# A four-layer graph network on one core: where layer 2's load buffers lie, and when the last row groups of layer 1 are updated

## The chip, the core and the metric

The kernel runs on one core of a Trainium2 chip. The core has five engines, each with a stream of instructions of its own: TensorE (PE) multiplies, VectorE (DVE), ScalarE (ACT) and GpSimd (POOL) work elementwise, SyncE (SP) issues most transfers. [...] The metric is the device time of one execution in microseconds (us), as a median of several runs.

## The reference

A graph of N = 2708 nodes has 128 features each (`x`) and a sparse weighted adjacency matrix (`adj`, about 16 neighbours a row). Four layers follow each other, each as `x = x + layer(relu(layernorm(x)), adj)`:

```python
h = jnp.maximum(_layernorm(x, axis=-1), 0.0)
x = x + _L0_gnn_ref(h, adj)          # H.T @ X, scaled by 1 / column sums
h = jnp.maximum(_layernorm(x, axis=-1), 0.0)
x = x + _L1_gnn_ref(h, adj, ...)     # sum over j of gelu(s_i + d_j + b) * adj[i, j], then an update
h = jnp.maximum(_layernorm(x, axis=-1), 0.0)
x = x + _L2_gnn_ref(h, adj, ...)     # adj @ states, a dense layer, a GRU cell
h = jnp.maximum(_layernorm(x, axis=-1), 0.0)
x = x + _L3_gnn_ref(h, adj, ...)     # masked attention with two heads
```

The end of layer 1, which matters here, is for every row

```python
combined = jnp.concatenate([node_feats, aggregated], axis=-1)
new_feats = combined @ upd_w.T + upd_b
h = jax.nn.gelu(new_feats, approximate=False) + node_feats
return (h - mu) / jnp.sqrt(var + LN_EPS) * ln_w + ln_b
```

and then the residual and the layer norm with relu that open layer 2.

## The kernel before

Rows lie in 22 tiles of 128 (the last has 20 rows), and the tiles in six groups: groups 0 to 4 have four tiles, group 5 (`LAST`) has tiles 20 and 21.

Layer 1 uses lists instead of the dense matrix. For every row and each of 22 column blocks the up to eight largest entries are kept: values in `val`, places in `col`. Each row tile then passes through a pipeline of *periods*, one period a tile, written out by hand: the order of instructions on each engine is the order of the calls. `period(t)` has six sub-steps `k` (`GB` = 6). In it PE multiplies for tile t (`combine`, `gather`), while DVE, POOL, ACT and SP prepare tiles t+1 to t+3. The steps named below:

- `pass_on` (line 826): PE transposes `where` (`p_w`), ACT copies it, SP writes it to memory and reads it back to every partition as `spread`.
- `columns` (836): DVE turns `spread` into `cols`, an operand of `combine`.
- `place` (line 773 to 679): DVE makes `where`, `value` and `mine` for the tile two ahead.
- `put_values` (805): POOL makes eight 128x128 blocks of `put`, an operand of `gather`; `put_more` (814): ACT makes the other fourteen.
- `activate` (899): ACT applies gelu to `combine`'s result and so frees its bank.
- `close_tile` (920 to 929): PE ends the tile's sum; after a group's last tile ACT copies it to `aggT`.

When a group's tiles are closed, `mix` (942, 943) multiplies the group's features and `aggT` by the update's weights into `p_u`, and `update` brings the group to the input of layer 2 in eight steps on alternating engines: 0 DVE adds the bias; 1 ACT gelu; 2 DVE adds the features and takes moments, POOL takes a power for the root (line 120); 3 DVE makes factors (126 to 130); 4 ACT scales (136), POOL multiplies and adds `ln_w`, `ln_b` (972); 5 DVE adds to `xs` and takes moments, POOL the power; 6 DVE makes factors; 7 ACT writes the rows of `h` (named `hs` in the profile) that layer 2 multiplies. Every group does one step a period, at sub-step 2, starting the period after its `mix`. So groups 3, 4 and 5 end after the last period: eight more rounds of `updates` follow period 22. Then come a check of the lists' lengths (`over`, `many`, lines 1092 to 1097) and the end of the hand-written order; the pools of layer 1 close, those of layers 2 and 3 open over the freed memory.

In layer 2, for each of six column chunks (512 columns wide, the last 148), SP loads the transposed adjacency (`adjT`) in five pieces of up to five row tiles into three rotating buffers `a` of pool `l2a` (lines 1334, 1336). DVE and POOL write from each piece the byte mask that layer 3 uses (1338, 1341), and PE adds the product with the rows of `h` (1346): 22 row tiles, two recorded products each, 44 a chunk. `finish_chunk` follows, interleaved with the next chunk by a small planner that counts units of PE time. A buffer is loaded again when its mask operations and products are done. Layer 3 runs its attention products on PE.

Memory: a pool gets its place when it opens, and what lies there was used by something else. The first load into a buffer waits for all earlier readers and writers of these bytes. In before, the three `a` buffers lie at bytes 167904 to 198624 of each partition, over the end of layer 1's working tiles: `aggT`, of which the last `mix` reads, lies from 166848 to 168896.

Of the kernel before, what the change touches and what calls it, by code (L numbers as in the profile page):

```python
# [20 lines left out]
F32 = mybir.dt.float32  # L21
# [9 lines left out]
P = 128  # L31
# [29 lines left out]
def listed_layers(ctx: ExitStack, tc: tile.TileContext, x, adj, w, out, flag):  # L61
# [76 lines left out]
    def tiles_of(v, t, k):  # L138
        return [v[:, t + q, :] for q in range(k)]
# [66 lines left out]
    lim = fix.tile([P, 4], F32, name="lim")  # L206
    wheres = [fix.tile([P, P], BF16, name=f"where{q}") for q in range(2)]
    msg_wT, upd_wT = (fix.tile(list(w[v].shape), F32, name=v) for v in ("msg_wT", "upd_wT"))
    upd_b, ln_w, ln_b, msg_b = (fix.tile([P, D], F32, name=v) for v in ("upd_b", "ln_w", "ln_b", "msg_b"))
    src_self = fix.tile([P, 2, D], F32, name="src_self")  # L210
    state = {}

# [259 lines left out]
            )  # L472

    def measure(g):
        state["m", g] = moments(tiles_of(xs, *GROUPS[g]), "n1")

    def rows(g):
        t, k = GROUPS[g]
# [5 lines left out]
    for s in range(1, RING):  # L484
        load_cut(0, s)
    nc.vector.tensor_scalar(offdiag, ident, -1.0, 1.0, ALU.mult, ALU.add)
    state["m", -1] = moments(tiles_of(xs, 0, 4), "n0")
    for q in range(2):
        nc.gpsimd.memset(wheres[q], 0.0)

# [49 lines left out]
    for i, (c, s) in enumerate(order):  # L540
        g0, gk = GROUPS[s]
        if i == len(order) - 1:
            for n in range(4):
                list_last(n)
            count_some(0, FIRST)
            count_some(FIRST, 1)
        list_cut(c, s, g0)
        if i == 0:
            state["f", 0] = factors(*state.pop(("m", -1)))
            list_cut(c, s, g0 + 1)  # L550
            state["m", 1] = moments(tiles_of(xs, *GROUPS[1]), "n0")
            list_cut(c, s, g0 + 2)
            state["f", 1] = factors(*state.pop(("m", 1)))
            list_cut(c, s, g0 + 3)
        else:
            for n in range(g0 + 1, g0 + gk):
                if c > 0 and s == (1 if c < LAST - 1 else 0) and n == g0 + 2:
                    invert(c - 1)
                list_cut(c, s, n)
        if i + 1 < len(order):  # L560
            mask_near(*order[i + 1])
        if i > 0 and i - 1 + RING < len(order):
            load_cut(*order[i - 1 + RING])
        if c == LAST - 2:
            load_cut(LAST, s)
        if c > 0 and s == (2 if c < LAST - 1 else 1):
            turn_sums(c - 1)
        if (c, s) == (LAST - 1, LAST):
            turn_rows(LAST - 2)
            ranked = rank(0, FIRST, bank("p_r"))  # L570
            turn_sums(LAST)
        work_cut(c, s, first_steps(s) if c == 0 else next_steps(c, s))
        if c > 1 and s == 0:
            turn_rows(c - 2)
        if c > 1 and s == 1:
            destinations(c - 2)
        if c > 1 and s == 3:
            split_destinations(c - 2)
        if c == LAST - 1:
            for z in PARTS.get(s, ()):  # L580
                mask_near(LAST, z)
                work_cut(LAST, z)
            if s == LAST - 1:
                for _ in lift(LAST):
                    pass

        if (c, s) == (0, 3):
            nc.sync.dma_start(msg_wT, w["msg_wT"])
            nc.sync.dma_start(upd_wT, w["upd_wT"])
            for v, name in ((upd_b, "upd_b"), (ln_w, "ln_w"), (ln_b, "ln_b"), (msg_b, "msg_b")):  # L590
                nc.sync.dma_start(v, w[name].partition_broadcast(P))
        if (c, s) == (2, 3):
            W_msgT, W_ihT, W_hhT = load(late, "W_msgT"), load(late, "W_ihT"), load(late, "W_hhT")
            b_msg, b_ih, b_hh = load_columns(late, "b_msg"), load_columns(late, "b_ih"), load_columns(late, "b_hh")
            ff0T, ff0, ff1T = load(late, "ff0T"), load(late, "ff0"), load(late, "ff1T")
            attn = load_columns(late, "attn")
            gain1, shift1, gain2, shift2 = (load_columns(late, v) for v in ("g1", "b1", "g2", "b2"))
            nc.gpsimd.tensor_copy(src_self[:, 0, :], msg_wT[:, 0, :])
            nc.gpsimd.tensor_tensor(src_self[:, 1, :], msg_wT[:, 0, :], msg_wT[:, 1, :], ALU.add)
# [60 lines left out]
    with (  # L660
# [284 lines left out]
        def update(g, step):  # L945
            t, k = GROUPS[g]
            if step == 0:
                u = work.tile([P, 4, D], F32, name="u1")
                if g not in mixed:
                    mix(g)  # L950
                if size(t + k - 1) < P:
                    nc.vector.memset(u[:, k - 1, :], 0.0)
                pv = mixed.pop(g).rearrange("p (t d) -> p t d", t=4)
                bv = upd_b.unsqueeze(1).to_broadcast([P, 4, D])
                whole = k if size(t + k - 1) == P else k - 1
                nc.vector.tensor_tensor(u[:, 0:whole, :], pv[:, 0:whole, :], bv[:, 0:whole, :], ALU.add)
                if whole < k:
                    nc.vector.tensor_tensor(u[0:TAIL, whole, :], pv[0:TAIL, whole, :], upd_b[0:TAIL, :], ALU.add)
                ups[g] = [u]
# [17 lines left out]
                scale_rows(tiles_of(h, t, k), tiles_of(xs, t, k), *ups[g].pop(), AF.Relu)  # L977
                ups.pop(g)

        def updates(t):  # L980

            for g, (first, k) in enumerate(GROUPS):
                step = t - (first + k + 1)
                if 0 <= step < STEPS:
                    update(g, step)

        GB = (NB + 3) // 4

        def period(t, between=()):

# [4 lines left out]
            for k in range(GB):  # L995
# [20 lines left out]
                if k == 1:  # L1016
                    if now and t % 2 == 0 and t + 2 < NT:
                        project(t // 2 + 1)
                    for g, (first, n) in enumerate(GROUPS):
                        if t == first + n + 1:  # L1020
                            mix(g)
                if k in (1, 2) and b:
                    fetch(t + 2, k - 1)
                if k == 1 and a:
# [1 line left out]
                if k == 2:  # L1026
                    if now and t % 2 == 0 and t + 2 < NT:
                        sources(t // 2 + 1)
                    if a:
                        select_rows(t + 3)  # L1030
                    if now and t + 4 < NT:
                        count_rows(t + 4)
                    updates(t)
                if k > 0 and c:
                    put_more(t + 1, k)
                if k == 3 and c:
# [43 lines left out]
        if True:  # L1080
            period(0)
            for t in range(1, NT + 1):
                period(t)
            for t in range(NT + 1, NT + 1 + STEPS):
                updates(t)
        ordered.close()
        puts.close()


        over = fix.tile([P, 2], F32, name="over1")  # L1090
        many = once.tile([P, NT, NB], BF16, tag="picked", name="many")
        nc.vector.tensor_tensor(many, ends, rows_n, ALU.add)
        nc.vector.tensor_scalar(many, many, float(E), None, ALU.is_gt)
        nc.vector.reduce_sum(over[:, 0:1], many, AX.XY)
        nc.vector.tensor_scalar(many, val[:, :, :, S - 1], 0.0, None, ALU.is_gt)
        nc.vector.reduce_sum(over[:, 1:2], many, AX.XY)
        nc.vector.tensor_tensor(flag, over[:, 0:1], over[:, 1:2], ALU.add)
    lists.close()


# [1 line left out]

    l3 = ctx.enter_context(tc.tile_pool(name="l3", bufs=1))
    h3 = l3.tile([P, NT, D], F32, name="h3")
    mask = l3.tile([P, NT, N], U8, name="mask")
    below = l3.tile([P, 2 * NT + 1], F32, name="below")
    nc.gpsimd.memset(below, 0.0)
    hv = l3.tile([P, NT, 2, D + 1], F32, name="hv")  # L1110
    lift = l3.tile([P, NT, 2], F32, name="lift")
    row = l3.tile([P, 2, N], F32, name="row")
    score = l3.tile([P, NT, 4], F32, name="score")
    nc.gpsimd.memset(score[:, NT - 1, :], 0.0)
    nc.gpsimd.memset(hv[:, NT - 1, :, :], 0.0)
    nc.gpsimd.memset(lift[:, NT - 1, :], 0.0)
    nc.gpsimd.memset(mask[:, NT - 1, :], 0)
    ident_8 = l3.tile([P, P], U8, name="ident_8")
    nc.vector.tensor_copy(ident_8, ident)
    PIECE = 5  # L1120
    RUNS = ((0, 3), (3, 8), (11, 8), (19, 3))
    MOST = 8
    accs = ctx.enter_context(tc.tile_pool(name="l23p", bufs=1, space=PSUM))


    clock = [0.0]
# [192 lines left out]
            yield apart  # L1319

    with (
        tc.tile_pool(name="l2a", bufs=3) as apool,
        tc.tile_pool(name="l2g", bufs=1) as pool,
        tc.tile_pool(name="l2z", bufs=2) as zpool,
        tc.tile_pool(name="l3v", bufs=4) as vpool,
        tc.manual_schedule(),
    ):
        def aggregate(t0, k0, pa, j0):

# [131 lines left out]

        for g, (t0, k0) in enumerate(GROUPS):
            pa = accs.tile([P, CH], F32, tag=f"acc{g % 2}", name="p_agg")
            for j0 in range(0, NT, PIECE):
                aggregate(t0, k0, pa, j0)
            if t0 == 0:
                late_weights()
            follow(finish_chunk(t0, k0, pa))
            advance()
        last = RUNS[0]  # L1470
        banks = products(last, (0, 1), vpool, 2)

    out_pool = ctx.enter_context(tc.tile_pool(name="l3o", bufs=2))

# [487 lines left out]
```

## Time and profile before

| what | us |
|---|---|
| median of three runs (1040.25 to 1042.27) | 1040.8 |
| the profiled execution | 1038.74 |
| its span, first to last instruction | 1036.9 |
| PE busy in the span | 925.8 |
| DVE busy | 798.5 |
| ACT busy | 533.0 |
| POOL busy | 470.7 |
| mean granted PE clock, as a share of full speed | 0.94 |

The profile's first lines give the busy share of each engine in 40 slices of about 26 us, in tenths (9 stands for 90% or more), then the granted clock of PE:

```profile
PE   5799898945999999999999779999978999999983
DVE  7999798977677888987774456666588977997793
ACT  5755656824666676676666312333322434654342
POOL 6322221422977789897875373344311300340042
PEclk9899899965899999999999789999989999999996
```

Layer 0 fills slices 1 to 9, layer 1 goes on to slice 22, layer 2 from there to slice 29, layer 3 takes the rest. Lines of a timeline give start, length, engine, source line, operation, output<-input, shapes and count of merged instructions; in brackets the engine's idle time before it and what ended it.

### The profile page before, as it was taken

How to read it: one execution, taken by the hardware profiler on the slowest of the kernel's cores; microseconds unless marked ns; L12 is line 12 of the kernel's file. 1: busy time of each engine (PE TensorE's matmuls, PEld its weight loads, DVE VectorE, ACT ScalarE, POOL GpSimd, SP SyncE). 2: the span in 40 equal slices, each digit the busy share in tenths (PEclk: the TensorE clock that was granted, in tenths of full speed). 3: DMA queues.
4: the chain of work that ended last, by engine and by line, in shares of the span. 5: the costliest groups of instructions: out<-in, count | busy, mean ns of one | idle time of the engine just before them, and what ended most of it. 6: DMA issues, size and time to landing. Idle time of an engine off the chain costs nothing. (4 is left out here: it accounts for less than half of the span.)

```text
span 1036.9 us, 22170 instructions
## 1 busy us (share of the span) xinstructions
PE 925.8 (89%) x7948; PEld 748.7 (72%) x7948; DVE 798.5 (77%) x2753; ACT 533.0 (51%) x1561; POOL 470.7 (45%) x588
## 2 busy tenths in 40 slices
PE   5799898945999999999999779999978999999983
PEld 3455455624999999999999634444578999989972
DVE  7999798977677888987774456666588977997793
ACT  5755656824666676676666312333322434654342
POOL 6322221422977789897875373344311300340042
PEclk9899899965899999999999789999989999999996
DMA  9799899512333342433221345566411467456100
GB/s 301 254 307 372 256 384 376 200 58 84 120 107 122 100 128 93 128 95 122 80 93 56 135 163 189 191 222 208 117 48 31 141 212 218 135 162 208 36 14 17
DMA packets 83194, 162.90 MB, mean 157 GB/s; under 512 B 14672, under 2 KB 30148, under 8 KB 83074
## 3 DMA queue, kind: packets, MB, share of 16 engines
q1 hardware_dynamic: 63094, 129.25, 38.5%
q10 hardware_dynamic: 19980, 32.14, 8.5%
q8 instruction: 64, 1.05, 0.4%
q14 instruction: 56, 0.46, 0.2%
HBM read 114.74 MB, written 30.87 MB: 140 GB/s over the span
## 5 line engine op out<-in xcount | busy, mean ns | idle before, releaser
L805 POOL TENSOR_SCALAR put<-count,line,value 128x128 f32<-128x128 f32 x176 | 200.0, 1149 | 32.8 <-DVE value L794 32.6
L1184 PE MATMUL att<-hv,wt 128*128 128x129 f32 x1672 | 195.9, 278 | 7.8 <-DVE wt L1154 6.3
L1184 PEld LDWEIGHTS att<-hv,wt 128*128 128x128 f32 x1672 | 192.2, 194 | 10.8 <-DVE wt L1154 7.0
L887 PE MATMUL p_m<-s,sel 128*128 128x128 bf16 x1452 | 163.3, 221 | 8.8 <-ACT g L899 6.3
L891 PE MATMUL p_m<-d,cols 124*128 124x128 bf16 (+1 forms) x1452 | 163.3, 221 | 2.9 <-DVE cols L836 2.9
L1154 DVE SCALAR_TENSOR_TENSOR wt<-row,lift,mask 128x1024 f32<-128x1024 f32 (+1 forms) x132 | 138.8, 1082 | 23.3 <-PE att L1184 23.3
L120 POOL TENSOR_TENSOR n_r<-n_r,minus_half 128x4 f32<-128x4 f32 (+1 forms) x28 | 39.9, 1425 | 233.3 <-DVE n_r L119 226.1
L912 PE MATMUL agg<-put,g 128*128 128x128 f32 (+1 forms) x968 | 123.1, 279 | 0.0
L1346 PE MATMUL p_agg<-a,hs 128*128 128x512 f32 (+2 forms) x264 | 110.4, 560 | 13.7 <-DMA a<-adjT 7.6
L380 PE MATMUL sums<-a,h 128*128 128x512 f32 x220 | 120.3, 644 | 1.6 <-ACT h L136 1.6
L394 PEld LDWEIGHTS p_T<-ident,a 128*128 128x128 f32 (+1 forms) x440 | 55.9, 147 | 81.5 <-issue 37.5
L912 PEld LDWEIGHTS agg<-put,g 128*128 128x128 f32 x968 | 113.7, 193 | 0.0
L887 PEld LDWEIGHTS <-sel 128*128 128x128 bf16 x1452 | 104.5, 98 | 10.7 <-issue 10.1
L891 PEld LDWEIGHTS <-cols 124*128 124x128 bf16 (+1 forms) x1452 | 103.7, 98 | 3.8 <-DVE cols L836 3.8
L814 ACT ACTIVATE put<-mine,value 128x128 f32<-128x128 bf16 x308 | 100.6, 392 | 0.0
L899 ACT ACTIVATE g<-p_m 128x512 f32<-128x512 f32 x132 | 72.8, 551 | 53.7 <-PE agg L912 41.2
L394 PE MATMUL p_T<-ident,a 128*128 128x128 f32 (+1 forms) x440 | 74.3, 290 | 26.8 <-ACT aT L399 20.2
L1346 PEld LDWEIGHTS p_agg<-a,hs 128*128 128x128 f32 (+1 forms) x264 | 48.0, 195 | 62.7 <-issue 53.1
L358 DVE FIND_INDEX8 col<-val,a 128x8 uint16<-128x124 f32 x342 | 92.0, 281 | 0.0
L356 DVE MAX8 val<-a 128x8 f32<-128x124 f32 x342 | 79.1, 272 | 8.3 <-DMA a<-in_adj 8.3
L399 ACT ACTIVATE aT<-p_T 128x512 f32<-128x512 f32 (+2 forms) x132 | 71.0, 539 | 26.5 <-PE p_T L394 25.4
L1307 ACT ACTIVATE hs<-hs 128x1354 f32<-128x1354 f32 (+1 forms) x44 | 58.4, 1329 | 48.5 <-DMA hs<-in_adj 48.1
(279 smaller groups left out, 1559.3 us busy)
## 6 DMA issues: line engine op xcount, KB each, us to landing
hs<-in_adj SPq DMA_DIRECT2D x42, 677.0 KB
adjT<-aT ACTq DMA_DIRECT2D x105, 256.0 KB
a<-adjT SPq DMA_DIRECT2D x20, 1280.0 KB
spread<-passed SPq DMA_DIRECT2D x22, 704.0 KB
later<-sel SPq DMA_DIRECT2D x22, 616.0 KB
a<-in_adj SPq DMA_DIRECT2D x5, 1152.0 KB
a<-in_adj SPq DMA_DIRECT2D x5, 1120.0 KB
a<-in_adj SPq DMA_DIRECT2D x5, 1088.0 KB
```

The costliest lines, as they stand in the source:

```text
L356: nc.vector.max(val[0:m, n, b, :], v)
L358: nc.vector.max_index(col[0:m, n, b, :], val[0:m, n, b, :], v)
L380: nc.tensor.matmul(accs[c][:, 0:w], h0[0:m, n, :], a[0:m, n - g0, t0 * P - lo : t0 * P - lo + w], start=(n == 0), stop=(n == NT - 1),)
L394: nc.tensor.transpose(p[0:k, i * iw + q * P : i * iw + q * P + m], a[0:m, q, e : e + k], ident[0:m, 0:m])
L805: nc.gpsimd.tensor_scalar(st["put", 0][:, b, :], count, st["line"][:, b : b + 1], st["value"][:, b : b + 1], ALU.is_equal, ALU.mult,)
L814: nc.scalar.activation(st["put", 1][:, b - HP, :], st["mine"][:, b - HP, :], AF.Identity, scale=st["value"][:, b : b + 1])
L887: nc.tensor.matmul(p[:, b - b0, :], st["sel"][:, b, :], s3[:, q, t % 2, :], start=(q == 0), stop=False)
L891: nc.tensor.matmul(p[:, b - b0, :], st["cols"][0:kb, b, :], d3[0:kb, b, q, :], start=False, stop=(q == 2))
L912: nc.tensor.matmul(agg, g[:, b - 4 * k, :], put, start=(b == 0), stop=False)
L1154: nc.vector.scalar_tensor_tensor(wt[:, 0:n], row[:, k, c : c + n], lift[:, j, k : k + 1], mask[:, j, c : c + n], op0=ALU.max, op1=ALU.mult,)
L1184: nc.tensor.matmul(banks[s // 3][:, s % 3, :], wt[:, q * P : (q + 1) * P], hv[:, j, k, :], start=(v < 2 and s // 3 not in touched), stop=( ...
L1346: nc.tensor.matmul(pa[:, 0:n], h[0:k, j, :], a[0:k, j - j0, 0:n], start=(j == 0), stop=(j == NT - 1))
```

## The change

1. The pools of layers 2 and 3 are placed anew. The tiles of layer 3 open at memory's far end (`side="right"`). The load buffers `a` now lie at bytes 52192 to 82912: the first wholly over `val`, the second over the end of `col` and over `later`, the third over the end of `val` and most of `col`. These pools and the PSUM pool `l23p` take `reuse_waits="tile"`. The biases `upd_b`, `ln_w`, `ln_b` move to a pool that lives on, and two sets of small tiles take the name "n4".
2. The list check moves to period 20, sub-step 1, as `check_lists`.
3. `mixes` and `updates` are tables over (period, sub-step). Groups 0 to 2 keep their places. Group 3 does a step every three sub-steps: period 17, sub-step 2, to period 20, sub-step 5. Group 4 is mixed in period 20 at sub-step 3, and does a step every sub-step from there to the end of period 21.
4. Group 5 has no place in the table. Its `mix` and step 0 stand before the first chunk's products, the rest between its five pieces: steps 1 and 2 after the first, 3 and 4 after the second, 5 after the third, 6 and 7 after the fourth. Its tile comes from layer 2's pool `l2z`.
5. Memsets of layer 3's last rows move into the first chunk (the mask's after the third piece, four small ones after the fifth). The hand-written order runs on to the end of layer 2.

```diff
-    upd_b, ln_w, ln_b, msg_b = (fix.tile([P, D], F32, name=v) for v in ("upd_b", "ln_w", "ln_b", "msg_b"))
+    upd_b, ln_w, ln_b = (late.tile([P, D], F32, name=v) for v in ("upd_b", "ln_w", "ln_b"))
+    msg_b = fix.tile([P, D], F32, name="msg_b")
...
-                u = work.tile([P, 4, D], F32, name="u1")
+                u = work.tile([P, 4, D], F32, name="u1") if g < LAST else zpool.tile([P, 4, D], F32, name="z3")
...
-        def updates(t):
-
-            for g, (first, k) in enumerate(GROUPS):
-                step = t - (first + k + 1)
-                if 0 <= step < STEPS:
-                    update(g, step)
-
         GB = (NB + 3) // 4
+        mixes, updates = {}, {}
+        for g, (first, n) in enumerate(GROUPS[:-1]):
+            at, apart = (first + n + 1) * GB + 1, GB
+            if g == LAST - 2:
+                apart = GB // 2
+            elif g == LAST - 1:
+                at, apart = at - GB + 2, 1
+            mixes[divmod(at, GB)] = g
+            for step in range(STEPS):
+                updates.setdefault(divmod(at + 1 + step * apart, GB), []).append((g, step))
+
+        def check_lists():
+            over = fix.tile([P, 2], F32, name="over1")
+            many = once.tile([P, NT, NB], BF16, tag="picked", name="many")
+            nc.vector.tensor_tensor(many, ends, rows_n, ALU.add)
+            nc.vector.tensor_scalar(many, many, float(E), None, ALU.is_gt)
+            nc.vector.reduce_sum(over[:, 0:1], many, AX.XY)
+            nc.vector.tensor_scalar(many, val[:, :, :, S - 1], 0.0, None, ALU.is_gt)
+            nc.vector.reduce_sum(over[:, 1:2], many, AX.XY)
+            nc.vector.tensor_tensor(flag, over[:, 0:1], over[:, 1:2], ALU.add)
...
-                    for g, (first, n) in enumerate(GROUPS):
-                        if t == first + n + 1:
-                            mix(g)
+                if (t, k) in mixes:
+                    mix(mixes[t, k])
...
-                    updates(t)
+                for g, step in updates.pop((t, k), ()):
+                    update(g, step)
+                if k == 1 and t == NT - 2:
+                    check_lists()
...
-            for t in range(NT + 1, NT + 1 + STEPS):
-                updates(t)
-        ordered.close()
+            assert not updates
         puts.close()
...
-    l3 = ctx.enter_context(tc.tile_pool(name="l3", bufs=1))
+    l3 = ctx.enter_context(tc.tile_pool(name="l3", bufs=1, side="right", reuse_waits="tile"))
...
-    accs = ctx.enter_context(tc.tile_pool(name="l23p", bufs=1, space=PSUM))
+    accs = ctx.enter_context(tc.tile_pool(name="l23p", bufs=1, space=PSUM, reuse_waits="tile"))
...
-        tc.tile_pool(name="l2a", bufs=3) as apool,
+        tc.tile_pool(name="l2a", bufs=3, reuse_waits="tile") as apool,
...
         for g, (t0, k0) in enumerate(GROUPS):
             pa = accs.tile([P, CH], F32, tag=f"acc{g % 2}", name="p_agg")
-            for j0 in range(0, NT, PIECE):
+            if g == 0:
+                update(LAST, 0)
+            for i, j0 in enumerate(range(0, NT, PIECE)):
                 aggregate(t0, k0, pa, j0)
-            if t0 == 0:
+                if g > 0:
+                    continue
+                for step in ((1, 2), (3, 4), (5,), (6, 7), ())[i]:
+                    update(LAST, step)
+                if i == 2:
+                    nc.gpsimd.memset(mask[:, NT - 1, :], 0)
+            if g == 0:
+                blank_rows()
+                nc.vector.tensor_copy(ident_8, ident)
                 late_weights()
             follow(finish_chunk(t0, k0, pa))
             advance()
         last = RUNS[0]
         banks = products(last, (0, 1), vpool, 2)
+    ordered.close()
```

More of the change, by code (lines that the diff above doesn't have):

```diff
@@ L474, in measure @@
     def measure(g):
-        state["m", g] = moments(tiles_of(xs, *GROUPS[g]), "n1")
+        state["m", g] = moments(tiles_of(xs, *GROUPS[g]), "n4")
     def rows(g):
@@ L486, in listed_layers @@
     nc.vector.tensor_scalar(offdiag, ident, -1.0, 1.0, ALU.mult, ALU.add)
-    state["m", -1] = moments(tiles_of(xs, 0, 4), "n0")
+    state["m", -1] = moments(tiles_of(xs, 0, 4), "n4")
     for q in range(2):
@@ L550, in listed_layers @@
             list_cut(c, s, g0 + 1)
-            state["m", 1] = moments(tiles_of(xs, *GROUPS[1]), "n0")
+            state["m", 1] = moments(tiles_of(xs, *GROUPS[1]), "n4")
             list_cut(c, s, g0 + 2)
@@ L1083, in listed_layers @@
                 period(t)
-            for t in range(NT + 1, NT + 1 + STEPS):
-                updates(t)
-        ordered.close()
+            assert not updates
         puts.close()
[L1090 to L1097, printed above, removed]
     lists.close()
-    l3 = ctx.enter_context(tc.tile_pool(name="l3", bufs=1))
+    l3 = ctx.enter_context(tc.tile_pool(name="l3", bufs=1, side="right", reuse_waits="tile"))
     h3 = l3.tile([P, NT, D], F32, name="h3")
@@ L1108, in listed_layers @@
     below = l3.tile([P, 2 * NT + 1], F32, name="below")
-    nc.gpsimd.memset(below, 0.0)
     hv = l3.tile([P, NT, 2, D + 1], F32, name="hv")
@@ L1113, in listed_layers, with blank_rows @@
     score = l3.tile([P, NT, 4], F32, name="score")
[L1114 to L1117, printed above, removed]
     ident_8 = l3.tile([P, P], U8, name="ident_8")
-    nc.vector.tensor_copy(ident_8, ident)
+    def blank_rows():
+        for v, to in ((below, 0.0), (score[:, NT - 1, :], 0.0), (hv[:, NT - 1, :, :], 0.0), (lift[:, NT - 1, :], 0.0)):
+            nc.gpsimd.memset(v, to)
     PIECE = 5
@@ L1321, in listed_layers @@
     with (
-        tc.tile_pool(name="l2a", bufs=3) as apool,
[L1323 to L1326, printed above, removed]
+        tc.tile_pool(name="l2a", bufs=3, reuse_waits="tile") as apool,
+        tc.tile_pool(name="l2g", bufs=1, reuse_waits="tile") as pool,
+        tc.tile_pool(name="l2z", bufs=2, reuse_waits="tile") as zpool,
+        tc.tile_pool(name="l3v", bufs=4, reuse_waits="tile") as vpool,
     ):
```

## The prediction

> **What bounds the kernel now.** I read in this order: the 40 slices, then a table of stretches over the seam between layers 1 and 2, then PE, the DMA queue and DVE in order of time. In the slices PE is at 9 tenths or more nearly everywhere and sags to 7 in slices 23 and 24, where the granted clock sags as well. That is the seam.
>
> ```profile
> 583.36:585.60 2.24, 2.13 (x9) 1.32 (x8) 1.52 (x6) 2.20 (x7) 0.00 (x0) 0.50 0.00 0
> 585.60:591.57 5.97, 0.00 (x1) 0.04 (x1) 3.81 (x21) 2.26 (x6) 1.81 (x2) 0.50 0.83 282
> 591.57:606.43 14.86, 14.86 (x30) 6.23 (x30) 11.44 (x30) 2.53 (x6) 11.28 (x13) 0.88 0.41 152
> 606.43:611.89 5.46, 0.00 (x0) 0.03 (x1) 1.88 (x7) 0.88 (x2) 4.12 (x4) 0.71 0.91 301
> 611.89:620.15 8.26, 8.26 (x15) 3.24 (x15) 2.58 (x6) 0.00 (x0) 5.44 (x3) 0.78 0.52 169
> ```
>
> Columns: stretch, its length, busy time of PE, weight load, DVE, ACT, POOL (with counts), granted clock, DMA share, GB/s. From the last product of layer 1 (583.36) to the end of layer 2's first chunk (620.15) pass 36.8 us: the update products `p_u` 2.2, a hole of 6.0, 30 aggregate products in 14.9, a hole of 5.5, the last 14 in 8.3. On both sides of this PE is full (20.00 of 20 us from 540 to 560, 25.82 of 26 from 620 to 646), so what the seam gains or loses moves the end.
>
> ```profile
> 585.56 1.52 SPq L1334 DMA_DIRECT2D a<-adjT  x3
> ...
> 591.57 8.85 PE L1346 MATMUL p_agg<-a,hs 128*128 128x512 f32 x16 [6.08 <-issue]
> ...
> 610.44 0.88 ACT L136 ACTIVATE hs<-xs,n_r 128x128 f32<-128x128 f32 x2 [10.11 <-DVE n_r L130]
> ...
> 611.89 8.26 PE L1346 MATMUL p_agg<-a,hs 128*128 128x512 f32 x14 [5.47 <-DMA a<-adjT]
> ...
> SPq L1334 <- PE p_u L943: 22.2, 1, 22.2
> ```
>
> The first hole: SP held the three load buffers' DMAs for 22.2 us until the last `p_u` product had read its operand, then issued all three; the first landed 6 us later. The second: load 4 was issued only at 605.92 (landed 611.8), and the `h` rows of group 5 were written only at 610.44.
>
> [...] clock 0.50 from 582 to 594, then 1.00; a product takes 0.44 us warm (30 in 13.23 from 633.80), the first 30 take 14.86. [...] Here a DVE mask took 3.35 us beside a POOL memset, 1.22 later; a POOL mask 2.8 beside DVE, 1.49 alone.
>
> **The change part by part.**
>
> *Loads.* In the changed program's order, load 1 waits for DVE's list check, which moves into period 20; loads 2 and 3 wait for the last `cols` on DVE and for POOL's `put` of tile 21. In before these ended by 555.7, 563.3 and 559.3; I reckon 562 and 569 below. A 1.28 MB load took 6 us, so all three land near 578, ahead of the first aggregate, and share no bytes with what PE still reads. The first hole's 6.0 us goes.
>
> *Group 5's update moves between the masks.* PE no longer stands behind the tail of groups 3, 4 and 5. With `p_u` ending at 590.9 (below): row of step 0 ends 591.5, gelu 592.0, mask 1 on DVE 1.6, step 2 1.5, POOL pow 595.3, mask 2, step 3 597.0, ACT 597.9, POOL's two 0.73 after its second mask 599.5, step 5 601.1, POOL mask and pow 603.0, DVE mask 4, step 6 607.0, ACT 607.9. PE wants these rows after 40 products, 590.9+14.9+10x0.44 = 610.2: slack 2.3 us. Load 4 follows PE's tenth product (597) and lands near 603, wanted at 605.8. Both parts of the second hole go, 5.5 us, and the last 14 products run warm: 14x0.44 = 6.2, 2.1 less.
>
> Sum of gains: 6.0+5.5+2.1 = 13.5 us with rounding. The first cold start I leave in (14.86).
>
> *Group 3 now does two steps a period.* Step 2 lands in period 18 ahead of `cols` and `place` on DVE. There DVE has no slack:
>
> ```profile
> 538.49 0.94 DVE L836 TENSOR_SCALAR cols<-spread,part 128x2816 bf16<-128x2816 bf16 x1
> ...
> 541.05 0.34 DVE L793 TENSOR_REDUCE where<-picked 128x22 bf16<-128x176 f32 x1
> ...
> 541.44 0.23 PE L822 MATMUL p_w<-ident_h,where 128*128 128x128 bf16 x1
> ```
>
> PE's `p_w` starts when `where` ends. Step 2 in before ran from 545.33 to 547.97, 2.64 us. PE waits that much: first for `cols`, then for `where`. Bounds: 1.5 (less if DVE drifts ahead) to 3.5 [...]. I take 2.6. Step 3 (0.9) follows `place` and is covered; in period 19 step 2 is gone from DVE, and step 5 comes after `place`. The list check (2.8 us) has DVE's idle 6.65 us before the last `cols` as cover.
>
> *Group 4's steps lie at every sixth of a period.* The mix moves 1.8 us of PE from period 21 to 20: zero. But step 7's four ACT rows now stand in ACT's queue before the two copies of `aggT` that PE's last `p_u` waits for. The chain of group 4 in before, from gelu to the last row, went hand to hand, each wait ended by its own last step:
>
> ```profile
> 583.63 0.64 ACT L963 ACTIVATE u<-u 128x512 f32<-128x512 f32 x1
> ...
> 590.77 1.27 POOL L972 TENSOR_TENSOR u<-u,ln_w 128x512 f32<-128x512 f32 x1 [2.75 <-ACT u L136]
> ...
> 598.68 1.65 ACT L136 ACTIVATE hs<-xs,n_r 128x128 f32<-128x128 f32 x4 [0.85 <-DVE n_r L130]
> ```
>
> 583.63 to 600.33 is 16.7 us. After: the gelu follows period 20's last activate (565.73, plus 2.6 for the stall, plus 1.8 for the mix: 570.1), its own 0.3 and group 3's step 7 (1.65): it starts at 572.1. It ends at 588.8, `aggT` at 589.2. PE wants `aggT` from 583.75+2.6 = 586.4. PE waits 2.7-2.8 us; I take 2.7. Bounds 0 and 5. Queued behind the ACT rows is only this copy; behind it PE's `p_u` and with it all of layer 2.
>
> *POOL.* Ahead of `put` of tile 21 now come group 3's two 128x512 operations (1.3 to 2.0 each) and two pows. `put` of 20 runs 545 to 554, these to 560.4, `put` of 21 to 567.4 or, at its 1.15 us each, 569.6. Its products start near 578: covered. The memsets of layer 3 (0.7 us and the mask's 2.41) move between masks; counted above.
>
> *One answer:* the late pool for biases, the shared "n4" names and the other tiles' new places add no instruction; waits behind the seam are the same or on things long done.
>
> Net: 13.5-2.6-2.7 = 8.2 us. Profiled execution 1038.7 (span 1036.9 and 1.8 around it) becomes 1030.5; the median lies 2.1 higher, so 1040.8 becomes 1032.6.
>
> **Rivals.**
> - *Both new stalls are hidden.* For: DVE and ACT are idle for long stretches from 555 on. Against: `where` and `p_w` touch. Gain 13.5: 1027.3. Chance 0.20.
> - *Group 5's chain stays late.* In before it took 24.4 us (586.9 to 611.3) amid the same masks; from 591.0 that ends at 615.4, 5.2 after PE's need, and the last 4 products run cold, 1.8. Gain 1.2: 1039.6. Against: half of the old 24 us went to waiting behind group 4 and two POOL masks in a row. Chance 0.07.
> - *It doesn't do what it says:* the loads still come late (a wait on a DMA or `put` that I place too early), so the first hole of 6.0 stays. 1038.6. Chance 0.05.
> - *Slower: POOL.* The pow of group 4's step 2 stands in POOL's queue behind `put` of 21. From 540 to 560 POOL is busy 17.45 of 20 us. I have it free at 569, wanted at 575.3; each microsecond beyond 575.3 delays step 7, `aggT` and the end by as much. From 8.2 us beyond, `put` ending after 583.5, the gain is gone; at 586 the time is 1043.3. Chance 0.06.
>
> **How the numbers follow.** The forecast (0.62) spans its bounds: best 13.5+1.6 (no cold start) less 1.5 and 0, 13.6 gained; worst 13.5-5.0-3.5-1.8, 3.2 gained: 1027.2 to 1037.6. With the hidden-stall rival inside, 1027 to 1037.6 leaves some 0.18 out. A difference under 0.2% (2.1 us) can't be told from none. Faster by more: 0.62+0.20 and half of the two middle rivals, 0.88. Same: the other half, 0.06. Slower: 0.06.
>
> **What would show it.** Right: loads 1 to 3 issued before 572, PE's gap before the first aggregate 2 to 3 us and charged to `aggT`, no hole between 15th and 16th row tile, 2 to 3 us of PE idle at the start of period 19, PE gapless up to the second chunk, which starts near 612. Wrong: a PE hole over 2 us inside the first chunk, loads issued after 580, POOL's `put` ending after 575, or a half clock lasting past 595.

## The result, and the profile after

The changed kernel took 1033.43 us (median of 4 runs, 1032.76 to 1034.53), the kernel before 1040.78 on the same chip: a ratio of 0.9928, 95% interval 0.9911 to 0.9945. That is 7.4 us less, where 8.2 were forecast. The profiled execution took 1032.76 us, its span 1031.0.

The two stretches of the seam that answer to the five of before, from the table of stretches of the changed kernel (stretch, length, busy time of PE, weight load, DVE, ACT, POOL with counts, granted clock, DMA share, GB/s):

```profile
587.52:592.78 5.26, 2.50 (x11) 1.54 (x10) 0.98 (x6) 1.87 (x6) 0.70 (x1) 0.69 0.00 0
592.78:613.83 21.05, 21.05 (x46) 8.86 (x45) 13.10 (x34) 2.18 (x5) 15.72 (x14) 0.91 0.46 143
```

The first stretch runs from the close of the last row tile of layer 1 to the first aggregate product, the second to the second chunk. In the second PE is busy all of the time: the hole between the 15th and the 16th row tile is gone. In the first PE is busy 2.50 of 5.26 us; what it waits for is in the order of time on PE and ACT (start, duration, operation; in brackets the idle time before it and who ended it):

```profile
587.84 0.49 PE L943 MATMUL p_u<-upd_wT,hT 128*128 128x128 f32 x2
591.09 0.79 PE L944 MATMUL p_u<-upd_wT,aggT 128*128 128x128 f32 x2 [2.76 <-ACT aggT L927]
...
592.78 21.11 PE L1348 MATMUL p_agg<-a,hs 128*128 128x512 f32 x44
```

```profile
589.24 1.65 ACT L136 ACTIVATE hs<-xs,n_r 128x128 f32<-128x128 f32 x4 [3.40 <-DVE n_r L130]
590.79 0.24 ACT L927 COPY aggT<-agg 128x128 f32<-128x128 f32 x1
```

The four `hs` rows are group 4's step 7. The copy of `aggT` stands behind them in ACT's queue, though PE finished what it copies at about 588: PE waits 2.76 us for a copy of 0.24. On SP's queue the load that waited for the last `p_u` in before is now early:

```profile
564.42 39.74 SPq L1336 DMA_DIRECT2D a<-adjT  x5
```

(The line joins five loads; the first was issued at 564.4, as the list check ended and 28 us ahead of its first product, the second and third at 569.7 and 570.1, as POOL's `put` of tile 21 ended.) The other wait of the forecast is 45 us earlier, at the start of period 19. DVE, then PE, of the changed kernel:

```profile
539.99 0.68 DVE L966 TENSOR_TENSOR u<-u,hs 128x512 f32<-128x512 f32 x1
...
542.51 0.95 DVE L837 TENSOR_SCALAR cols<-spread,part 128x2816 bf16<-128x2816 bf16 x1
...
545.08 0.34 DVE L794 TENSOR_REDUCE where<-picked 128x22 bf16<-128x176 f32 x1
```

```profile
543.51 0.34 PE L892 MATMUL p_m<-d,cols 124*128 124x128 bf16 x3 [2.25 <-DVE cols L837]
...
545.47 0.29 PE L823 MATMUL p_w<-ident_h,where 128*128 128x128 bf16 x1 [0.60 <-DVE where L794]
545.55 0.53 PE L888 MATMUL p_m<-s,sel 128*128 128x128 bf16 x3
```

`u<-u,hs` is the head of group 3's step 2. It and its statistics hold DVE from 539.99 to 542.51, `cols` follows, and PE waits 2.25 and 0.60 us, first for `cols` and then for `where`. Behind the wait the same three products take 0.53 us, not 0.33: the granted clock, 1.00 from 541 to 545, is 0.53 from 545 to 548, which the forecast did not have. The clock fell in a second place too, where both kernels have the same wait. Before, then after:

```profile
506.37 0.33 PE L887 MATMUL p_m<-s,sel 128*128 128x128 bf16 x3 [1.84 <-ACT g L899]
...
507.05 2.00 PE L912 MATMUL agg<-put,g 128*128 128x128 f32 x16
```

```profile
506.62 0.33 PE L888 MATMUL p_m<-s,sel 128*128 128x128 bf16 x3 [1.84 <-ACT g L900]
...
507.29 3.40 PE L913 MATMUL agg<-put,g 128*128 128x128 f32 x16
```

Sixteen products take 2.00 us before and 3.40 after, behind 1.84 us of waiting each; the granted clock from 507 to 510 is 1.00 before and 0.61 after. Both kernels hold the same work there.

To sort what follows I cut PE's time in each profile at four events: A, the product behind that wait near 506; B, the close of the last row tile of layer 1 (`agg<-ident,gs` of 20 rows); C, the first aggregate product; D, the first product of the second chunk (`p_w<-attn,ff`). All differences are worked out from these starts.

| us between the events | A to B | B to C | C to D | A to D |
|---|---|---|---|---|
| before | 76.38 | 8.82 | 28.51 | 113.71 |
| after | 80.90 | 5.26 | 21.05 | 107.21 |
| difference | +4.52 | -3.56 | -7.46 | -6.50 |
| forecast | +2.6 | -6.0+2.7 = -3.3 | -5.5-2.1 = -7.6 | -8.3 |

(The forecast's 8.2 was 13.5 less 5.3, with rounding.) B to C and C to D came out within 0.3 us. What was missed lies all in A to B.

### The profile page after: what moved, and what is told of

The parts are those of the page before. It is cut to its first block, busy times and chain, and to the rows that moved or that the text cites. A ratio compares the mean times of both kernels' runs of the same rounds, so it can differ in the third digit from the quotient of the medians.

```text
span 1031.0 us, 22163 instructions
## 1 busy us (share of the span) xinstructions
PE 922.2 (89%) x7948; PEld 747.7 (73%) x7948; DVE 797.4 (77%) x2753; ACT 532.7 (52%) x1561; POOL 470.9 (46%) x588
## 5 line engine op out<-in xcount | busy, mean ns | idle before, releaser
L806 POOL TENSOR_SCALAR put<-count,line,value 128x128 f32<-128x128 f32 x176 | 197.6, 1136 | 32.8 <-DVE value L795 32.6
```

What stands on the lines that cost most here:

```text
L806: nc.gpsimd.tensor_scalar(st["put", 0][:, b, :], count, st["line"][:, b : b + 1], st["value"][:, b : b + 1], ALU.is_equal, ALU.mult,)
```

## The experiments

All times are ratios to the kernel before on the same chip, with 95% intervals. Up to A the kernels below hold the same work, yet A lies between 506.2 and 510.9 in their profiles; so of the profile it is the stretches from A on that compare.

| kernel | ratio | A to B | B to C | C to D | A to D |
|---|---|---|---|---|---|
| changed kernel again | 0.9912 (0.9894 to 0.9929) | 79.55 | 5.27 | 21.10 | 105.92 |
| group 3's step 2 behind `place` | 0.9925 (0.9909 to 0.9940) | 78.06 | 5.09 | 20.88 | 104.03 |
| group 4's rows behind `aggT` | 0.9890 (0.9871 to 0.9909) | 78.73 | 1.71 | 20.97 | 101.41 |
| these two together | 0.9867 (0.9850 to 0.9884) | 79.83 | 1.71 | 19.28 | 100.82 |
| group 3's step 2 behind `sel` | 0.9883 (0.9861 to 0.9905) | 76.00 | 4.87 | 21.68 | 102.55 |
| that, with the rows behind `aggT` | 0.9846 (0.9824 to 0.9869) | 75.56 | 2.66 | 21.31 | 99.53 |
| the same again | 0.9859 (0.9842 to 0.9875) | 76.08 | 2.66 | 20.93 | 99.67 |
| that, and the last tile's gather wide | 0.9855 (0.9839 to 0.9872) | 75.73 | 1.71 | 19.27 | 96.71 |
| the same again | 0.9842 (0.9810 to 0.9875) | 75.72 | 1.70 | 19.28 | 96.70 |
| loads late again | 0.9993 (0.9982 to 1.0004) | 79.69 | 11.86 | 21.17 | 112.72 |
| early loads alone | 0.9989 (0.9979 to 1.0000) | 75.61 | 2.66 | 34.60 | 112.87 |

**The changed kernel once more**, with no edit.

> The changed kernel once more, unedited. Its first profile shows two drops of the TensorE clock that my sum left out: after a wait of 1.84 us near 506 us (the kernel before has the same wait and kept the full clock), and after the new wait of 2.85 us at the start of period 19 (products in 0.53 us, not 0.33). Theory: the first is chance, so in this profile the clock near 506 may well stay full and the span be 1.6 us shorter than 1031.0; the second follows from a longer wait and comes back. Rival: both come with the change, the clock near 506 drops again and the span is within 0.5 us of 1031.0. Time 1033.4, within 1.

The median was 1031.67 us, 1.7 below the first and so outside what I expected (1033.4 within 1); the ratios' intervals overlap. The wait near 506 was there (1.84 us), the clock behind it stayed full (1.00 from 507 to 510), and A to B is 1.35 us shorter than in the first profile; 3.40 less 2.00 is 1.4. Of thirteen profiles (before and twelve others), each with a wait of 1.8 us there, only the first of the changed kernel shows the drop. So it does not come with the change; what brought it there, the runs don't show. The drop at the start of period 19 came back (0.50 from 545 to 548). Without the first drop A to D is 7.79 us shorter than before, against 8.3 forecast. The span did not follow: it is 1030.7, 0.3 us shorter and not the 1.6 expected. This profile reached A 0.7 us later, and 0.3 us went behind D.

**Group 3's step 2 behind `place`.** The steps from 2 on are called at slots of their own:

```diff
+            slots = [divmod(at + 1 + step * apart, GB) for step in range(STEPS)]
+            if g == LAST - 2:
+                slots[2:] = ((18, 4), (19, 4), (19, 5), (20, 4), (20, 5), (21, 1))
             for step in range(STEPS):
-                updates.setdefault(divmod(at + 1 + step * apart, GB), []).append((g, step))
+                updates.setdefault(slots[step], []).append((g, step))
```

> Group 3's steps 2 to 7 are called at other places: step 2 after the placing of rows in period 18, not ahead of it, the others one period later or so. My theory: the 2.85 us wait of PE at the start of period 19 goes, and the half clock behind it (1.4 us) with it: 1029.2 (2.6 to 5 us less than 1033.4). Rival 1: PE waits there for something else on DVE or POOL as well, so that the wait only changes its name: 1033.4 within 1. Rival 2: the wait is shifted to aggT, since group 4's chain does not move: its wait grows from 2.76 to above 5 us and the time stays within 1 of 1033.4.

1031.91 us, no less than the unedited kernel beside it (1031.67). The first rival was right: the wait changed its name. DVE, then PE, of this kernel:

```profile
543.97 0.68 DVE L966 TENSOR_TENSOR u<-u,hs 128x512 f32<-128x512 f32 x1
...
546.50 1.63 DVE L750 TENSOR_TENSOR sel<-sel,later 128x2816 bf16<-128x2816 bf16 x1
```

```profile
542.50 0.23 PE L823 MATMUL p_w<-ident_h,where 128*128 128x128 bf16 x1 [0.49 <-DVE where L794]
...
548.18 0.44 PE L761 MATMUL y<-xb,sel 128*128 128x37 bf16 x11 [2.48 <-DVE sel L750]
```

The waits for `cols` and most of that for `where` are gone, and PE waits 2.48 us for `sel` instead, the last DVE operation of that period that PE reads. A to B is 1.49 us shorter than in the unedited profile: the clock did not fall this time (1.00 from 541 to 554), and the timed runs do not show this gain. The forecast's "DVE has no slack" holds for more of the period than it had looked at.

**Group 4's rows behind the copies of `aggT`.**

```diff
+            slots = [divmod(at + 1 + step * apart, GB) for step in range(STEPS)]
+            if g == LAST - 1:
+                slots[7] = (NT, 1)
...
```

> Group 4's step 7 (four ACT rows, 1.65 us in all) is called behind the copies of the last aggT, not ahead of them. My theory: the copies need only PE's close of tile 21 (587.5 in the profile of the changed kernel), so aggT is there at 588.2, the wait of 2.76 us shrinks to under 0.6, and the time falls by 2.2 to 2.8: 1031.0. Rival: the close of tile 21 or group 5's chain ends later than I think and takes the wait's place (a hole before the last row tiles of the first chunk instead): 1033.4 within 0.7.

1028.41 us, 3.3 below the unedited kernel on the same chip, a little more than expected. The intervals of the two ratios overlap, so the size is better read from the profile. ACT, then PE:

```profile
587.76 0.27 ACT L927 COPY aggT<-agg 128x128 f32<-128x128 f32 x1 [2.11 <-PE agg L921]
587.92 0.18 ACT L928 COPY aggT<-agg 128x20 f32<-128x20 f32 x1
589.05 1.65 ACT L136 ACTIVATE hs<-xs,n_r 128x128 f32<-128x128 f32 x4 [0.95 <-DVE n_r L130]
```

```profile
588.08 0.49 PE L944 MATMUL p_u<-upd_wT,aggT 128*128 128x128 f32 x2
...
589.04 21.04 PE L1351 MATMUL p_agg<-a,hs 128*128 128x512 f32 x44
```

The copy starts when PE's close ends, and the bracket at `p_u` is gone. B to C falls from 5.27 to 1.71 us: 2.76 of wait, and 0.8 because `p_u` now runs ahead of the clock's fall and not behind it (its two products on `aggT` take 0.49 us, not 0.79). Nothing takes the wait's place: the 44 products still run without a hole. The second stall of the forecast is shown, in place and size.

**Both**, with group 3's rows moved behind the copies too.

> Both edits, with group 3's rows behind the copies of aggT as well. If the two waits stand one after the other on PE's path, as my sum has it, the gains add: 1026.8 (1025 to 1028.5), which would be the shortest of all. Rival: they overlap (PE's arriving earlier after the first edit only lengthens another wait ahead of the first chunk): not below the better of the two single edits by more than 1 us.

1026.63 us, as expected, but not for the reason given. The wait for `sel` was there again, with a drop of the clock behind it (0.60 from 551 to 554), and C to D was short because here the clock did not fall at the end of layer 1 (1.00 from 578 to 602):

```profile
549.23 0.44 PE L761 MATMUL y<-xb,sel 128*128 128x37 bf16 x11 [2.48 <-DVE sel L750]
...
590.01 19.34 PE L1353 MATMUL p_agg<-a,hs 128*128 128x512 f32 x44
```

**Group 3's step 2 behind `sel`.** Against the first edit of group 3:

```diff
-                slots[2:] = ((18, 4), (19, 4), (19, 5), (20, 4), (20, 5), (21, 1))
+                slots[2:] = ((18, 5), (19, 4), (19, 5), (20, 4), (20, 5), (21, 1))
```

> As the first edit of group 3, but step 2 one slot later, behind the last DVE operation on sel in period 18 too. In the earlier run PE's wait of 2.85 us did not go, it changed from cols to sel (2.48 us). New theory: DVE has no idle time from 535 to 551 us, so whatever stands behind step 2 there is late; behind sel it stands in front of DVE's pause and the wait goes (under 0.8 us in all from 537 to 560), the products stay at 0.33: 2.5 to 4.3 us less than the unedited changed kernel: 1028.5 (1027.5 to 1030.5). Rival: cols of period 19 takes its place, the wait comes a third time, at 551 to 556, and the time stays within 1 of the first edit's (1031.9).

1029.66 us, inside what was expected. DVE of this kernel:

```profile
544.33 1.62 DVE L750 TENSOR_TENSOR sel<-sel,later 128x2816 bf16<-128x2816 bf16 x1
545.87 0.69 DVE L966 TENSOR_TENSOR u<-u,hs 128x512 f32<-128x512 f32 x1
...
549.30 0.95 DVE L837 TENSOR_SCALAR cols<-spread,part 128x2816 bf16<-128x2816 bf16 x1
```

Step 2 stands between `sel` and the `cols` of the next period, where DVE would pause. PE's waits over 0.3 us from 537 to 575 are 0.71 and 0.50 us, and no product is slow (the clock is 1.00 throughout). A to B falls to 76.00, 3.55 us below the unedited profile: PE is idle there for 1.20 us instead of 3.33, and the rest is put down to the clock (1.00 from 545 to 548, 0.50 in the unedited profile). The unedited kernel ran on another chip and the two ratios' intervals overlap, so this too rests on the profile. The stall at the start of period 19 is shown. The `aggT` wait stays at 1.84 us, since the rows are still ahead of the copy.

**That place and the rows behind `aggT`**: group 3's step 2 behind `sel`, and the ACT rows of groups 3 and 4 behind the copies; run on two chips.

> This place for group 3's step 2, and the ACT rows of groups 3 and 4 behind the copies of the last aggT. Theory: both waits gone, and no more than one drop of the clock between 500 and 590: 1023.8 (1022.5 to 1025.5), 2 to 4 us below the combination run before (1026.6). Rival (cols of period 19 late): 1026.6 within 1.

> The best combination once more, unedited, as the partner of the next run on the same chip. In its first profile PE has no gap of over 0.5 us from 543 to 586, and yet the clock falls to half at 583.4, in the last 28 products of layer 1 (20 columns each), and stays there for some 6.5 us: the 44 aggregate products take 21.4 us; where it did not fall (the first combination) they took 19.3. Theory: [...] the time is 1025.4 within 1.5, and this profile may or may not show it. Rival: it falls every time.

1025.39 and 1026.45 us, A to D 99.53 and 99.67. Both waits are gone at once, so they stood one after the other, as the sum had it. The gain over before is 14.2 us from A to D; the forecast's sum of gains without its two stalls is 13.5. The first median lies just inside what I expected (1022.5 to 1025.5), the second 1 us above that range, but within the 1.5 us given for it. The clock fell at the end of layer 1 in both profiles (0.50 from 584 to 587 in the first, from 587 to 590 in the second), as the rival of the second run had it.

**The last tile's gather wide.** On top of that, the last row tile of layer 1 gathers all 128 columns of `put` and not its 20; the other 108 are not used.

```diff
+            m = P
             agg = aggs[t // 4][:, t % 4, 0:m]
             g = st.pop(("g", k))
```

> The same, but layer 1's last tile gathers 128 columns, not its 20 (the other 108 are not used). Theory: the narrow products let the clock fall; 44 full ones cost 44 x (0.125 - 0.116) = 0.4 us more and keep it, the cold stretch from 582 to 592 goes (1.8 us): 1.4 us less than the partner. Rival: the width of the products has nothing to do with it, the clock falls as before: 0 to 0.5 us more than the partner.

> The wide gather once more, unedited: its first profile kept the full clock through the end of layer 1 and the first chunk (44 products in 19.3 us), which of the ten profiles with the narrow one only one did. Theory (narrow products let the clock fall): full clock there again, ratio to before about 0.985. Rival (chance): the clock falls to half between 578 and 592 as in the others, 44 products in 21 us or more.

PE with the narrow gather, then with the wide one (first profile of each):

```profile
580.17 3.25 PE L913 MATMUL agg<-put,g 128*128 128x20 f32 x28
583.36 0.61 PE L921 MATMUL agg<-ident,gs 20*128 20x20 f32 x2
...
586.02 21.38 PE L1353 MATMUL p_agg<-a,hs 128*128 128x512 f32 x44
```

```profile
578.62 3.34 PE L914 MATMUL agg<-put,g 128*128 128x128 f32 x28
581.89 0.39 PE L922 MATMUL agg<-ident,gs 20*128 20x20 f32 x2
...
583.60 19.34 PE L1354 MATMUL p_agg<-a,hs 128*128 128x512 f32 x44
```

The wide products cost 0.09 us more, and in both profiles the clock stays full through layer 1's end (1.00 from 578 to 602); with the narrow ones it fell there, or within 10 us, in ten of eleven, to 0.50 to 0.53 over 3 us (in four of the ten it fell within PE's wait for `aggT`, of 2.58 to 2.77 us). A to D is 96.7 in both, 2.9 us below the narrow partner. In the timed runs the two can't be told apart: 1025.1 against 1026.45 on one chip, and intervals that overlap. So two profiles show the clock staying full; that this shortens the kernel, the measured times leave open.

**The loads late again.** A DVE memset of one column in each of the three load buffers, behind group 5's step 0, holds the loads back until the last `p_u` is read; the order of the updates stays as in the changed kernel.

```diff
+        held = []
...
-            a = apool.tile([P, PIECE, CH], F32, name="a2")
+            a = held.pop(0) if held else apool.tile([P, PIECE, CH], F32, name="a2")
...
             if g == 0:
                 update(LAST, 0)
+                for q in range(3):
+                    held.append(apool.tile([P, PIECE, CH], F32, name="a2"))
+                    nc.vector.memset(held[q][:, 0, 0:1], 0.0)
```

> The changed kernel with the loads late again: a DVE memset of one column of each of the three buffers, behind group 5's step 0, holds load 1, 2 and 3 back until the last p_u has been read. Theory: the first hole of the kernel before comes back, 6 us between the last p_u and the first aggregate product, and nothing else takes it up: 1038.9 (1037.5 to 1040.5). Rival: the order of the updates made the gain and the loads are mostly hidden behind group 5's chain: 1033 to 1035.

1039.9 us: the gain is gone (0.9993), 1 us above the 1038.9 expected and inside its range. SP's queue, then PE:

```profile
592.42 17.45 SPq L1338 DMA_DIRECT2D a<-adjT  x5
```

```profile
598.37 21.24 PE L1350 MATMUL p_agg<-a,hs 128*128 128x512 f32 x44 [6.51 <-DMA a<-adjT]
```

The first load is issued at 592.4 and PE waits 6.51 us for it. B to C grows by 6.59 us, the other stretches move by 0.14 or less. The first hole is shown, in size too. The gain of the new order from C to D is still there (21.17 us, 28.51 in before); its own two stalls, with the clock, and the hole take it back in A to B and B to C.

**The early loads alone.** The memory layout of the change, with the updates as before: one step a period, the rest in a block behind the last period and ahead of the masks, group 5's too. Group 5's tile lies with those of the other groups again.

```diff
-        for g, (first, n) in enumerate(GROUPS[:-1]):
-            at, apart = (first + n + 1) * GB + 1, GB
...
+        for g, (first, n) in enumerate(GROUPS):
+            mixes[first + n + 1, 1] = g
             for step in range(STEPS):
-                updates.setdefault(divmod(at + 1 + step * apart, GB), []).append((g, step))
+                updates.setdefault((first + n + 1 + step, 2), []).append((g, step))
...
-            assert not updates
+            for slot in sorted(updates):
+                for g, step in updates[slot]:
+                    update(g, step)
...
-                for step in ((1, 2), (3, 4), (5,), (6, 7), ())[i]:
-                    update(LAST, step)
```

> The early loads alone: the updates in the order of the kernel before (one step a period, the rest in a block behind the last period, ahead of the masks). Theory: no hole before the first product, no wait at the start of period 19 and none for aggT by group 4's rows, but the first masks stand behind the block on DVE, so load 4 is issued near 603 and PE stands still for 6 to 9 us after the 30th product: second chunk from 616, 1036.5 (1034.5 to 1039). Rival: the early loads are the whole gain, the order of the updates only trades waits: 1031 to 1033.

1040.18 us (0.9989), 3.7 more than I expected and above the range (1034.5 to 1039); the mechanism is the expected one. PE, then DVE:

```profile
585.38 14.87 PE L1345 MATMUL p_agg<-a,hs 128*128 128x512 f32 x30
611.06 8.99 PE L1345 MATMUL p_agg<-a,hs 128*128 128x512 f32 x14 [10.81 <-DMA a<-adjT]
```

```profile
603.52 4.51 DVE L1337 TENSOR_SCALAR mask<-a 128x2048 uint8<-128x2048 f32 x3 [0.32 <-issue]
610.95 1.97 DVE L1337 TENSOR_SCALAR mask<-a 128x2048 uint8<-128x2048 f32 x2 [2.92 <-DMA a<-adjT]
```

PE starts 6.2 us earlier (B to C 2.66 against 8.82) and stands still 10.81 us after its 30th product instead of 5.5: the first masks come behind the block at 603.5, load 4 waits for the first of them, is issued at 605.1, where I expected it near 603, and lands at 610.9. C to D is 6.09 longer than before. The first hole went and came back in the second. None of the stalls of the changed order is there (A to B 75.61). What the new place, `reuse_waits` and the earlier list check each have in the early loads was not tried apart.

## Why the prediction came out as it did

It was right in direction and mechanism, and 0.8 us off in the median. A second set of runs of the same kernel gained 8.7 us. That it came so near is in part two errors that offset each other from A to B, as the missing term below shows. By its own steps:

- *Loads.* "All three land near 578" and the first hole's 6.0 us goes: load 1 was issued at 564.4, and holding the loads back brings 6.6 us back.
- *Group 5's update between the masks.* 5.5 and 2.1 us of gain were forecast, C to D fell by 7.46; the 44 products took 21.11 us, forecast 14.9 and 6.2. The last rows were written at 610.2 where PE wanted them near 612.1 (592.78+21.11-4x0.44): 1.9 us of slack, forecast 2.3.
- *The sum of gains* adds what does not all add: from A to D the early loads alone bring 0.84 us, though the sum gives their hole 6.0, since the hole comes back ahead of the fourth piece. The new order with late loads brings 0.99, where the sum leaves 2.2 (8.2 less 6.0); 0.7 of the rest lies in A to B, where the clock fell (0.56 from 545 to 548). Both together bring 7.79 (in the profile without the drop near 506). The working treats the holes as one seam, so the sum is right, but it doesn't say that neither part would have shown alone.
- *Group 3's step 2.* 2.6 us forecast, 2.85 measured. Moving it behind `sel` leaves 0.5 of it.
- *Group 4's rows.* 2.7 forecast, 2.76 measured. Moving them behind `aggT` takes it away. Both ends of this wait came 1.8 to 1.9 us later than forecast: PE wanted `aggT` at 588.3 (forecast 586.4), and it was there at 591.0 (forecast 589.2), so the length held.
- *The missing term* is the clock behind the new wait. "I take 2.6", and its bound of 3.5, counted the idle time alone. From A to B PE is idle for 1.22 us in before, one wait for ACT's `g` at 537.4, and for 3.18 and 3.33 us in the two profiles of the changed kernel: 2.0 and 2.1 more, less than the 2.6 forecast, because that wait for `g` shrank to 0.33 and 0.48. Half clock, estimated as half of the time that the traces show at 0.50, cost 0.66 us there in before, at the end of layer 1, and 3.41 and 1.71 after; the first of these holds 1.7 for the drop behind the wait near 506. The two differences add up to 4.7 and 3.2 us, and A to B grew by 4.52 and 3.17.
- *The clock in before* was read too kindly. The working has a "cold start" behind the first hole, but in before the clock fell at 581.4 (0.72 from 581 to 582, then 0.50), 4 us ahead of that hole and within layer 1's last products. What came before it is in the last section.
- *A sign of being wrong* that the prediction named did show: a half clock past 595. It lasted to about 596.4 (0.50 from 595 to 596, 0.81 from 596 to 597): the seam came some 2 us later than forecast, and the clock fell only near 589.6 (0.78 from 589 to 590), within the `aggT` wait. The time it costs is inside the forecast's 14.9 for 30 products.
- *Rivals.* POOL's `put` of tile 21 ended at 569.7 (forecast 567.4 or 569.6), 8 us ahead of the pow behind it, which ran at 578.1; the slower case was far off. Group 5's chain was in time, the loads were early. "Both stalls hidden" is what the best combination makes true: its forecast 1027.3 stands against 1025.4 and 1026.5.

## What to carry to other kernels

Early loads and an earlier use of their buffers are one change: early loads alone only move the hole to the next load, and what the new order alone gains goes on its own stalls and the first hole. Work moved into a full period belongs behind the last operation of that engine which the bound engine still reads in that period, not merely behind the first one that would be late; on ACT, work that nobody needs soon belongs behind a short copy that the bound engine waits for. A wait of PE can cost more than itself: behind 2.5 to 2.9 us of it at the start of period 19 the clock fell in five of six profiles, and in the sixth, where it did not, A to B was 1.49 us shorter than in the unedited profile (next section).

## What the runs showed of the hardware that was not expected

The granted clock fell behind some waits of PE and not behind others. Behind the wait of 1.8 us near 506 it fell in one of thirteen profiles (0.61 from 507 to 510 in the changed kernel's first, 1.00 in before). Behind 2.5 to 2.9 us at the start of period 19 it fell in five of six (to between 0.50 and 0.60 over 3 us). The same wait of 2.48 us for `sel`, first with group 3's step 2 behind `place`, then with both first edits together (stretches of 3 us; PE, weight load, DVE, ACT, POOL, granted clock, DMA share, GB/s):

```profile
545.00:548.00 3.00, 0.70 (x7) 0.51 (x5) 2.84 (x9) 0.60 (x1) 1.33 (x1) 1.00 0.64 240
548.00:551.00 3.00, 2.82 (x62) 2.82 (x63) 1.91 (x8) 1.78 (x8) 3.00 (x3) 1.00 0.00 0
551.00:554.00 3.00, 3.00 (x40) 2.99 (x38) 2.83 (x7) 1.99 (x7) 3.00 (x5) 1.00 0.02 5
```

```profile
545.00:548.00 3.00, 1.75 (x17) 1.56 (x14) 2.79 (x12) 0.60 (x1) 0.28 (x1) 1.00 0.54 195
548.00:551.00 3.00, 1.77 (x30) 1.78 (x31) 2.77 (x7) 0.86 (x4) 3.00 (x2) 0.83 0.11 45
551.00:554.00 3.00, 3.00 (x43) 3.00 (x42) 1.19 (x4) 1.57 (x5) 3.00 (x5) 0.60 0.02 5
```

In the first the wait ends at 548.18, the clock stays full, and groups of three products behind it take 0.33 us. In the second it ends at 549.23, the clock falls, and from 550.03 such groups take 0.53 us. Why one wait had the drop behind it and the other not, the runs don't show.

The clock also fell where PE was busy for the whole stretch, in or within some 2 us behind the 28 products of 20 columns at the end of layer 1: in before (0.57 from 581 to 584), with the early loads alone (0.68 there), and in four profiles of edited kernels (0.88 and 0.89 there, 0.69 from 584 to 587, 0.90 from 587 to 590). PE was busy for 3.00 of 3.00 us in each of these stretches. With the same products in the first combination it did not fall (1.00 from 578 to 602), and with 128 columns it did not in two of two (1.00 from 578 to 602). What decides, these runs don't show.
